# Grouped cross-attention: spreading maxima and sums by VectorE's transposes, and normalising one step later

## The chip, the cores and the metric

The kernel runs on one core of a Trainium2 chip. The metric is the device time in microseconds (us) of one execution; the median of three runs is given. A profile of a further execution gives the order of time on each engine: TensorE (PE, with its weight loads as PEld), VectorE (DVE), ScalarE (ACT), GpSimd (POOL) and the DMA queues.

## The reference

Four cross-attention layers follow each other on a state `x` of 4 batches x 512 queries x 256 channels, with one context of 4 x 1024 keys x 512 channels; everything is float32. Layers 0, 2 and 3 are "masked": 16 heads of 64, logits scaled by 1/8, with 20 subtracted from two pairs of key columns for the queries that a mask names. Layer 1 is "grouped": a norm of the queries, 16 query heads of 16, four of which share one of 4 key heads.

```python
# layers 0, 2, 3
logits = jnp.einsum('bhqd,bhkd->bhqk', q, k) * scale + col_bias[None, None, :, :]
out = jnp.einsum('bhqk,bhkd->bhqd', softmax(logits), v)
x = out.transpose(...).reshape(B, HW, 1024) @ Wo + bo + x
# layer 1
q = (rmsnorm(x, norm_w) @ wq).reshape(B, T, 16, 16); k, v = cond @ wk, cond @ wv   # 4 heads of 16
scores = jnp.einsum('btgrd,bsgd->bgrts', qg, k) * 0.25
x = x + einsum('bgrts,bsgd->btgrd', softmax(scores), v).reshape(B, T, 256) @ wo
```

## The kernel before, in words

**Units and steps.** Each layer of each batch is cut into 8 units, so there are 96 masked and 32 grouped units. A masked unit is two heads; its logits, transposed (keys on partitions, queries along the free dimension), are 8 tiles of 128 keys x (2 heads x 512 queries). A grouped unit is four query heads' half: two of the four sharing groups, its logits again 8 tiles of 128 x 1024. Its index `h` is 0 ("even") or 1 ("odd"); an even and the following odd unit share one output tile `gq[b, "o"]` of 128 x 512. The order is written out by hand in two strings: 96 steps, each with one masked unit `g`, and in 32 of them one grouped unit `lam` as well. The grouped units of a batch stand in eight steps on end; the four batches' runs of eight are apart. In the code of a step, `coming` is the grouped unit of the next step, `follows` the masked one, `g1` the masked unit of the step before.

**One step in order.** `scores(g)` makes the 8 masked logit tiles (L653, one with the mask product L659), ScalarE copies each to SBUF (L663), and VectorE keeps a running maximum in PSUM (L667). `max_quarters` turns and reduces that maximum to one value for each query (L713, L721, L738). With a grouped unit, `reciprocal_sums(g1)` then sums the exponentials of `g1` over the keys and makes its reciprocals (L713 again, L810 to L821). Then four rounds follow on TensorE: two key blocks of `attend(g1)` (L685), then `exponentials_pair(lam, i)`, which is two grouped logit tiles (L617, "pair i") whose exponentials ScalarE takes straight from PSUM (L640). `scale_out(g1)` multiplies the output by its reciprocals (L830), `max_everywhere` spreads the masked maximum over the partitions (L745), and VectorE subtracts it from the 8 tiles (L750), ScalarE exponentiates (L756), GpSimd sums (L795). Beside these, a list `fill` gives TensorE the projections of queries (L549), outputs (L845), keys (L473) and values (L515), attention of the grouped unit (`attend_grouped`), and, between them, the logits of `coming` for its maximum only (`maxima_pair`, L617 with L607 and L609). A step without a grouped unit attends to `g1` in one go after `max_everywhere` and then goes to its list, outputs first. Each engine runs its instructions in the order in which the code issues them.

**The grouped maximum.** After the last of the four `maxima_pair`s, `max_columns` reduces the maxima to columns `mcol` (L713, L721, L730). In the next step, after six of the eight masked score tiles, `lower_queries(lam)` spreads them by 16 products with the identity (L630), and VectorE puts them, negated, into the row of the queries that meets a row of ones in the keys (L635). The grouped logits then come out already lowered by their maximum.

**The grouped sums.** The values carry a column of ones at place 16 of each 32, so the output tile has its sums in row 16 of each 32. At the end of a step with an odd unit, `sums_grouped` spreads these rows by a product with `sel` (L705); `normalise_grouped` turns them, takes reciprocals, turns them back and multiplies (L571 to L573 in `reciprocal_rows`, L800). Its output is projected in the next step.

**PSUM banks.** PSUM's eight banks are handed out by a small class `Place` when the code is built, for one bank or for an aligned pair. Each bank carries the count of returns at which it was last given back; a bank taken is deleted from the dictionary, a bank returned is put at its end with the newest count. A pair goes by the later of its two counts. A single bank goes by this rule:

```python
at = min(free, key=lambda n: free[n] + (2 if n ^ 1 in free else 0))
```

A bank's next user must wait for the last reader of the one before. Pair 0 of the grouped logits takes two aligned pairs while the masked maximum still holds a third and the output of `attend(g1)` one bank of the fourth.

Of the kernel before, what the change touches and what calls it, by code (L numbers as in the profile page):

```python
# [12 lines left out]
ALU = mybir.AluOpType  # L13
# [3 lines left out]
P = 128  # L17
B, S, C = 4, 512, 256
T, CT = 1024, 512
NI = S // P  # L20
NT = T // P
# [55 lines left out]
def kernel(ctx: ExitStack, tc: tile.TileContext, a: dict, out: bass.AP):  # L77
    nc = tc.nc
# [7 lines left out]
    def t_(shape, tag, name, bufs=1, dtype=FP):  # L86
        return sb.tile(shape, dtype, tag=tag, name=name, bufs=bufs)
# [31 lines left out]
    def st_slot(n):  # L119
        return st_all[:, n // (NT + 1), n % (NT + 1), :]  # L120
# [4 lines left out]
    ident = t_([P, P], "ident", "ident")  # L125
# [2 lines left out]
    nc.vector.memset(ones, 1.0)  # L128
    eps = t_([P, 1], "eps", "eps")
    nc.vector.memset(eps, EPS)  # L130

    sel = t_([P, 4, 32], "sel", "sel")
    nc.vector.tensor_copy(
        sel, ident.rearrange("p (g d) -> p g d", d=32)[:, :, 16:17].to_broadcast([P, 4, 32])
    )


    row16 = t_([P, 2], "row16", "row16")
    nc.vector.reduce_sum(
# [316 lines left out]
    gq = {}  # L456
# [108 lines left out]
    def reciprocal_rows(out_, in_, room):  # L565


        turned = room[:, 0:S]
        short = t_([P, S // 32, 1], "short", f"short{len(turns)}")
        turns.append(0)  # L570
        nc.vector.transpose(turned, in_)  # L571
        nc.vector.reciprocal(short, turned.rearrange("p (c r) -> p c r", r=32)[:, :, 0:1])
        nc.vector.transpose(  # L573
            out_.rearrange("p (c r) -> p c r", r=32), short.to_broadcast([P, S // 32, 32])
        )
# [44 lines left out]
                )  # L620
        return ws

    def lower_queries(g):

        w = Place(1)
        m = w.ap
        for n in range(NI):
            for c in range(4):
                column = NI * (c % 2) + n
                nc.tensor.matmul(  # L630
                    m[32 * c : 32 * (c + 1), n * P : (n + 1) * P],
                    lhsT=g.mcol[:, column : column + 1].to_broadcast([P, 32]), rhs=ident,
                    start=True, stop=True,
                )
        nc.vector.scalar_tensor_tensor(g.qt, m, row16[:, 1:2], g.qt, ALU.mult, ALU.add)  # L635
        w.back()

    def exponentials_pair(g, i):
        for odd, w in enumerate(logits_pair(g, i)):
            nc.scalar.activation(g.st[2 * i + odd], w.ap, AF.Exp)  # L640
            w.back()

    def scores(g, within):
        g.st = [st_slot((NT + 1) * g.ring + t) for t in range(NT)]
        g.mx = st_slot((NT + 1) * g.ring + NT)
        g.mx_place = Place()
        for t in range(NT):

            w = Place() if t else g.mx_place
            m = w.ap  # L650
            keys = slice(t * P, (t + 1) * P)
            for j in range(2):
                nc.tensor.matmul(  # L653
                    m[:, j * S : (j + 1) * S], lhsT=g.kt[g.rows[j], keys], rhs=g.qt[g.rows[j], :],
                    start=True, stop=t > 0,
                )
            if t == 0:
                for j in range(2):
                    nc.tensor.matmul(  # L659
                        m[:, j * S : (j + 1) * S], lhsT=aug_k[g.l][g.rows[j], keys],  # L660
                        rhs=aug_q[g.rows[j], :], start=False, stop=True,
                    )
            nc.scalar.copy(g.st[t], m)  # L663
            if t:
                w.back()
                top = g.mx_place.ap
                nc.vector.tensor_tensor(top, top, g.st[t], ALU.max)  # L667
            if t == 5:
                within()

    def place_out(g, width=1):
        g.place = Place(width)
# [26 lines left out]
        nc.vector.tensor_tensor(half, half, g.po[64:128, :], ALU.add)  # L699
        g.place.back()  # L700

    def sums_grouped(g):
        g.place = Place(1)
        g.psum = g.place.ap
        nc.tensor.matmul(  # L705
            g.psum, lhsT=sel.rearrange("p g d -> p (g d)"), rhs=gq[g.b, "o"], start=True, stop=True
        )

    def over_quarter(out_, of, op):
        nc.vector.tensor_reduce(  # L713
            out_, of.rearrange("p (b x) -> p b x", x=32), AX.X, op, apply_transpose=True
        )
# [5 lines left out]
        nc.vector.tensor_tensor(half, quarter[0:64, :], quarter[64:128, :], ALU.max)  # L721
        return half

    def max_columns(g):

        half = max_halves(g, g.mx)
        g.mcol = t_([P, 2 * NI], "mcol", f"mcol_{g.name}", bufs=3)
        of = half.rearrange("x (c h) -> x h c", h=4)
        for h in range(4):
            nc.vector.tensor_tensor(  # L730
                g.mcol[32 * h : 32 * (h + 1), :], of[0:32, h, :], of[32:64, h, :], ALU.max
            )

    def max_quarters(g):
        half = max_halves(g, g.mx_place.ap)
# [6 lines left out]
    def max_everywhere(g):  # L742
        g.mb_place = Place()
        g.mb = g.mb_place.ap
        nc.vector.transpose(  # L745
            g.mb.rearrange("p (b r) -> p b r", r=32), g.every.to_broadcast([P, 2 * S // 32, 32])
        )
# [46 lines left out]
    def running_sum(g, t):  # L794
        nc.gpsimd.tensor_tensor(g.acc, g.st[0] if t == 1 else g.acc, g.st[t], ALU.add)  # L795

    def normalise_grouped(g, room):
        g.ot = t_([P, S], "ot", f"ot_{g.name}", bufs=3)
        reciprocal_rows(g.ot, g.psum, room)
        nc.vector.tensor_tensor(g.ot, gq[g.b, "o"], g.ot, ALU.mult)  # L800
        g.place.back()

    def reciprocal_sums(g):

        w = Place(1)
        quarter, half = w.ap[:, 0:32], w.ap[0:64, 32:64]
        other = t_([64, 32], "other", f"other_{g.name}")
        short = t_([P, S // 32, 1], "short", f"short_{g.name}")
        over_quarter(quarter, g.acc, ALU.add)
        nc.vector.tensor_copy(other, quarter[64:128, :])  # L810
        nc.vector.tensor_tensor(half, quarter[0:64, :], other, ALU.add)
        nc.vector.tensor_copy(other[0:32, :], half[32:64, :])
        for h in range(4):
            cols = slice(h // 2 * S // 32, (h // 2 + 1) * S // 32)
            nc.vector.tensor_tensor(
                short[32 * h : 32 * (h + 1), :, 0], half[0:32, cols], other[0:32, cols], ALU.add
            )
        w.back()
        nc.vector.reciprocal(short, short)
        g.ot = t_([P, S], "ot", f"ot_{g.name}", bufs=3)  # L820
        nc.vector.transpose(  # L821
            g.ot.rearrange("p (c r) -> p c r", r=32), short.to_broadcast([P, S // 32, 32])
        )
# [81 lines left out]
    def at(n):  # L905
        return steps[n] if 0 <= n < len(steps) else (None, None)
# [32 lines left out]
    g0, g1 = masked[0:2]  # L939
# [23 lines left out]
    attended = None  # L963
    count = 0
    ready = []
    left = {b: 32 - 4 for b in range(B)}

    for n in range(len(steps) + 2):
        g, lam = at(n)
        follows, coming = at(n + 1)  # L970
        soon = at(n + 2)[1]
        g1, attended = attended, g
# [42 lines left out]
        def pair(i):  # L1015
            if i == 0:
                behind_exponentials()
            maxima_pair(coming, i)
            if i == NT // 2 - 1:
                max_columns(coming)  # L1020

        if coming:
            share(coming)
# [12 lines left out]

        if g:
            g.now = NT if masked_at(g.n + 1) else 4
            scores(g, lambda: lower_queries(lam) if lam else None)

        ending = n >= len(steps) - 2
        if g1 and (g or lam):
# [1 line left out]
        if g:  # L1044
            max_quarters(g)
            if not lam:
                g.mx_place.back()
                max_everywhere(g)
        if lam:
            if g1:  # L1050
                reciprocal_sums(g1)
            for i in range(NT // 2):
                if g1:
                    attend(g1, range(2 * i, 2 * i + 2))
                if coming and not g:
                    pair(i)
                exponentials_pair(lam, i)
                if i == 0 and g:
                    g.mx_place.back()
                if not g:  # L1060
                    if i == 1 and outs:
                        project_out(outs.pop(0))()
                    if i == 2 and queries:
                        project_q(queries.pop(0))()
            if g1:
                scale_out(g1)
                ready.append(g1)
            if g:
                max_everywhere(g)
        elif g1 and g:  # L1070
            attend(g1)
            if not ending:
                late.append(lambda: normalise(g1))
        elif g1:
            attend_last(g1)
            adds = [project_out(each) for each in outs]
            outs = []
            reciprocal_rows(g1.ot, g1.psum, g1.mx)
            scale_out(g1)
            for add in adds:  # L1080
                add()
# [71 lines left out]
        while pairs:  # L1153
            pair(pairs.pop(0)[1])
        behind_exponentials()
        if coming and not follows:
            lower_queries(coming)
        if lam and lam.h == 1:
            sums_grouped(lam)
            normalise_grouped(lam, st_slot((NT + 1) * (count % 2) + NT))  # L1160
            ready.append(lam)
        if g1 and g1 not in ready:
            ready.append(g1)
# [30 lines left out]
```

## Time and profile before

| what | value |
|---|---|
| median of 3 runs | 3775.26 us (3774.84 to 3775.55) |
| profiled execution | 3773.92 us, span 3772.2 us from the first to the last instruction |
| mean granted TensorE clock | 0.998 |
| busy share: TensorE, VectorE, ScalarE, GpSimd | 99%, 80%, 56%, 43% |
| DMA | 98.71 MB, mean 26 GB/s |

In the profile a group's line gives the line of code, engine, operation, tiles (out<-in) and sizes, then the count, busy time and the mean of one in ns. An fp32 product stands as two matmul records for each product in the code. TensorE's matmuls overlap in the records, so the cost of a block on TensorE is read from its start to the start of what follows.

### The profile page before, as it was taken

To read this page: it belongs to the slowest core of one execution; us is meant where nothing else is said; L and a number is where in the kernel's file an instruction comes from. 1 tells how busy PE (TensorE), PEld (TensorE's weight loads), DVE (VectorE), ACT (ScalarE), POOL (GpSimd) and SP (SyncE) were. 2 spreads that over 40 slices of the span, in tenths; PEclk is the share of its full clock that TensorE was granted. 3 is DMA by queue.
4 is the path that set the end of the run, shared out by engine and by line. 5 is a ranking of instruction groups with operands and counts; after the bars stand their busy time and mean duration, and the time that the engine had idled before them with its cause. 6 is when DMAs were issued, how large, how long until landed. Compare 5 with 4: busy or idle time off the path is not lost.

```text
span 3772.2 us, 50461 instructions
## 1 busy us (share of the span) xinstructions
PE 3723.8 (99%) x19662; PEld 1860.2 (49%) x19662; DVE 3000.4 (80%) x3928; ACT 2104.1 (56%) x2433; POOL 1625.0 (43%) x749
## 2 busy tenths in 40 slices
PE   8999999999999999999999999999999999999998
PEld 4555544445444444444555555554544445555554
DVE  6887787877887778787888888888787778888888
ACT  4555555555555555555555555555555555555554
POOL 3555333343333433333555555555333335555554
PEclk9999999999999999999999999999999999999999
DMA  2111110001000010000000110000100000000100
GB/s 68 42 31 28 39 28 21 18 20 25 22 19 21 12 33 19 22 21 18 26 26 26 43 42 24 25 26 22 26 19 23 20 24 26 26 26 26 31 25 8
DMA packets 187875, 98.71 MB, mean 26 GB/s; under 512 B 43241, under 2 KB 183529, under 8 KB 187637
## 3 DMA queue, kind: packets, MB, share of 16 engines
q1 hardware_dynamic: 182510, 82.90, 8.0%
q0 software_dynamic: 2560, 8.39, 0.8%
q10 hardware_dynamic: 2566, 4.20, 0.5%
q8 instruction: 155, 2.54, 0.3%
q14 instruction: 84, 0.68, 0.1%
HBM read 89.16 MB, written 2.10 MB: 24 GB/s over the span
## 4 chain that ended last, share of the span: by engine, by line
PE 86%; DVE 9%; issue 2%; ACT 2%; DMA 0%; DVEq 0%; POOL 0%; ACTq 0%; POOLq 0%
PE ps L515 19%; PE ps L685 18%; PE ps L473 17%; PE ps L653 12%; PE ps L617 7%; DVE ps L667 6%; PE ps L845 5%; PE ps L549 5%; ACT st L663 2%; DVE st L750 1%; PE ps L491 1%; DVE qt L635 1%; PE ps L659 1%; PE ps L705 0%; PE ps L379 0%
## 5 line engine op out<-in xcount | busy, mean ns | idle before, releaser
L795 POOL TENSOR_TENSOR st<-st 128x1024 f32<-128x1024 f32 x668 | 1580.5, 2366 | 2088.3 <-ACT st L756 2044.0
L667 DVE TENSOR_TENSOR ps<-ps,st 128x1024 f32<-128x1024 f32 x672 | 828.2, 1232 | 462.8 <-ACT st L663 405.5
L756 ACT ACTIVATE st<-st 128x1024 f32<-128x1024 f32 x768 | 783.0, 1054 | 650.0 <-DVE st L750 636.2
L750 DVE TENSOR_TENSOR st<-st,ps 128x1024 f32<-128x1024 f32 x768 | 885.9, 1214 | 3.3
L685 PE MATMUL ps<-st,v 128*64 128x512 f32 x4064 | 810.9, 598 | 0.0
L663 ACT COPY st<-ps 128x1024 f32<-128x1024 f32 x768 | 716.1, 1044 | 107.3 <-PE ps L659 82.3
L515 PEld LDWEIGHTS ps<-wv,ctx 128*128 128x128 f32 x6400 | 729.4, 192 | 80.9 <-issue 64.6
L515 PE MATMUL ps<-wv,ctx 128*128 128x128 f32 x6400 | 744.8, 276 | 0.6 <-ACT st L663 0.6
L653 PE MATMUL ps<-qt,kt 64*128 64x512 f32 x3072 | 710.5, 598 | 0.0
L473 PE MATMUL ps<-ctx,wk 128*128 128x512 f32 x1536 | 693.3, 599 | 2.2 <-ACT ctx L385 2.2
L685 PEld LDWEIGHTS ps<-st,v 128*64 128x64 f32 x4064 | 231.2, 130 | 551.5 <-issue 491.6
L473 PEld LDWEIGHTS ps<-ctx,wk 128*128 128x128 f32 x1536 | 285.7, 190 | 395.7 <-issue 375.0
L653 PEld LDWEIGHTS ps<-qt,kt 64*128 64x128 f32 x3072 | 282.7, 186 | 323.8 <-ACT st L663 142.2
L527 ACT COPY v<-ps 128x512 f32<-128x512 f32 x200 | 117.2, 586 | 538.2 <-PE ps L515 538.1
L609 DVE TENSOR_TENSOR st<-st,ps 128x1024 f32<-128x1024 f32 x224 | 273.5, 1221 | 128.1 <-ACT st L607 70.7
L640 ACT ACTIVATE st<-ps 128x1024 f32<-128x1024 f32 x256 | 248.1, 1021 | 180.2 <-PE ps L617 139.8
L617 PE MATMUL ps<-qt,kt 32*128 32x512 f32 x2048 | 302.6, 639 | 16.1 <-DVE qt L635 12.8
L845 PE MATMUL ps<-ot,wo 128*128 128x512 f32 x448 | 214.6, 607 | 0.7 <-DVE ot L830 0.7
L549 PE MATMUL ps<-x,wq 128*128 128x512 f32 x384 | 185.5, 606 | 1.1 <-ACT x L357 1.1
L617 PEld LDWEIGHTS ps<-qt,kt 32*128 32x128 f32 x2048 | 91.0, 183 | 191.0 <-ACT st L640 52.2
L478 ACT COPY kt<-ps 128x512 f32<-128x512 f32 x192 | 110.3, 574 | 102.8 <-PE ps L473 102.6
L845 PEld LDWEIGHTS ps<-ot,wo 128*128 128x128 f32 x448 | 79.8, 189 | 129.2 <-issue 120.0
(143 smaller groups left out, 1629.9 us busy)
## 6 DMA issues: line engine op xcount, KB each, us to landing
wk<-in_L_xattn_Wk_dram SPq DMA_DIRECT2D x96, 256.0 KB, 2.9
wv<-in_L_xattn_Wv_dram SPq DMA_DIRECT2D x96, 256.0 KB, 2.7
wq<-in_L_xattn_Wq_dram SPq DMA_DIRECT2D x96, 128.0 KB, 2.8
wo<-in_L_xattn_Wo_dram SPq DMA_DIRECT2D x96, 128.0 KB, 2.9
qt<-qt ACTq DMA_DIRECT2D x32, 128.0 KB, 2.2
xraw<-in_x_dram SPq DMA_DIRECT2D x3, 512.0 KB
out_dram<-out SPq DMA_DIRECT2D x3, 512.0 KB
wq<-in_L_xattn_wq_dram SPq DMA_DIRECT2D x32, 32.0 KB, 3.4
```

The costliest lines, as they stand in the source:

```text
L473: nc.tensor.matmul(m, lhsT=g.wk[:, k, :], rhs=ctx_t[g.b][:, k, n * 512 : (n + 1) * 512], start=(k == 0), stop=(k == KT - 1),)
L515: nc.tensor.matmul(m[:, t * P : (t + 1) * P], lhsT=ctx_t[g.b][:, k, (4 * n + t) * P : (4 * n + t + 1) * P], rhs=g.wv[:, k, :], start=(k == ...
L549: nc.tensor.matmul(m, lhsT=g.wq[:, k, :], rhs=x[:, k, :], start=(k == 0), stop=(k == KC - 1))
L617: nc.tensor.matmul(ws[odd].ap[:, j * S : (j + 1) * S], lhsT=g.kt[rows, i * P : (i + 1) * P], rhs=g.qt[rows, :], start=True, stop=True,)
L653: nc.tensor.matmul(m[:, j * S : (j + 1) * S], lhsT=g.kt[g.rows[j], keys], rhs=g.qt[g.rows[j], :], start=True, stop=t > 0,)
L663: nc.scalar.copy(g.st[t], m)
L667: nc.vector.tensor_tensor(top, top, g.st[t], ALU.max)
L685: nc.tensor.matmul(g.po[at, :], lhsT=g.v[:, t, rows], rhs=g.st[t][:, j * S : (j + 1) * S], start=(t == first), stop=(t == last),)
L750: nc.vector.tensor_tensor(g.st[t], g.st[t], g.mb, ALU.subtract)
L756: nc.scalar.activation(st, st, AF.Exp)
L795: nc.gpsimd.tensor_tensor(g.acc, g.st[0] if t == 1 else g.acc, g.st[t], ALU.add)
L845: nc.tensor.matmul(m[:, k * S : (k + 1) * S], lhsT=g.wo[:, k * P : (k + 1) * P], rhs=g.ot, start=True, stop=True,)
```

## The change

The 16 products of the lowering and the product of the sums are taken out, with the tile `sel`. `lower_queries` absorbs `max_columns`: the maxima are put into a tile `every` of 128 x 16 and a VectorE transpose of its broadcast spreads them into a PSUM bank; the lowering of the queries follows at once, now at the end of the step before (after the last `maxima_pair`). `normalise_grouped` turns the output tile itself into a PSUM bank, takes the reciprocals of column 16 of each 32, turns them back into the same bank and multiplies from there. It no longer runs at the end of the odd unit's step: the unit goes into a list `turned`, which the next step empties behind `max_quarters` and, where there is a grouped unit, `reciprocal_sums(g1)`.

```diff
-    def max_columns(g):
+    def lower_queries(g):
         half = max_halves(g, g.mx)
-        g.mcol = t_([P, 2 * NI], "mcol", f"mcol_{g.name}", bufs=3)
-        of = half.rearrange("x (c h) -> x h c", h=4)
-        for h in range(4):
+        every = t_([P, S // 32, 1], "every1", f"every1_{g.name}")
+        for c in range(4):
+            cols = slice(c % 2 * S // 32, (c % 2 + 1) * S // 32)
             nc.vector.tensor_tensor(
-                g.mcol[32 * h : 32 * (h + 1), :], of[0:32, h, :], of[32:64, h, :], ALU.max
+                every[32 * c : 32 * (c + 1), :, 0], half[0:32, cols], half[32:64, cols], ALU.max
             )
+        w = Place(1)
+        m = w.ap
+        nc.vector.transpose(
+            m.rearrange("p (b r) -> p b r", r=32), every.to_broadcast([P, S // 32, 32])
+        )
+        nc.vector.scalar_tensor_tensor(g.qt, m, row16[:, 1:2], g.qt, ALU.mult, ALU.add)
+        w.back()
...
-    def normalise_grouped(g, room):
+    def normalise_grouped(g):
+        o = gq[g.b, "o"]
+        w = Place(1)
+        m = w.ap
+        short = t_([P, S // 32, 1], "short", f"short_{g.name}")
+        nc.vector.transpose(m, o)
+        nc.vector.reciprocal(short, m.rearrange("p (c r) -> p c r", r=32)[:, :, 16:17])
+        nc.vector.transpose(
+            m.rearrange("p (c r) -> p c r", r=32), short.to_broadcast([P, S // 32, 32])
+        )
         g.ot = t_([P, S], "ot", f"ot_{g.name}", bufs=3)
-        reciprocal_rows(g.ot, g.psum, room)
-        nc.vector.tensor_tensor(g.ot, gq[g.b, "o"], g.ot, ALU.mult)
-        g.place.back()
+        nc.vector.tensor_tensor(g.ot, o, m, ALU.mult)
+        w.back()
...
             if i == NT // 2 - 1:
-                max_columns(coming)
+                lower_queries(coming)
...
-            scores(g, lambda: lower_queries(lam) if lam else None)
+            scores(g)
...
             if not lam:
                 g.mx_place.back()
                 max_everywhere(g)
+        if lam and g1:
+            reciprocal_sums(g1)
+        for each in turned:
+            normalise_grouped(each)
+        turned.clear()
         if lam:
-            if g1:
-                reciprocal_sums(g1)
             for i in range(NT // 2):
...
         if lam and lam.h == 1:
-            sums_grouped(lam)
-            normalise_grouped(lam, st_slot((NT + 1) * (count % 2) + NT))
+            turned.append(lam)
             ready.append(lam)
```

More of the change, by code (lines that the diff above doesn't have):

```diff
@@ L130 @@
     nc.vector.memset(eps, EPS)
[L132 to L135, printed above, removed]
     row16 = t_([P, 2], "row16", "row16")
@@ L621, in logits_pair @@
         return ws
[L623 to L636, printed above, removed]
     def exponentials_pair(g, i):
@@ L641, in exponentials_pair, with scores @@
             w.back()
-    def scores(g, within):
+    def scores(g):
         g.st = [st_slot((NT + 1) * g.ring + t) for t in range(NT)]
@@ L667, in scores @@
                 nc.vector.tensor_tensor(top, top, g.st[t], ALU.max)
-            if t == 5:
-                within()
     def place_out(g, width=1):
@@ L700, in keep_odd @@
         g.place.back()
[L702 to L707, printed above, removed]
     def over_quarter(out_, of, op):
@@ L965 @@
     ready = []
+    turned = []
     left = {b: 32 - 4 for b in range(B)}
@@ L1155 @@
         behind_exponentials()
-        if coming and not follows:
-            lower_queries(coming)
         if lam and lam.h == 1:
-            sums_grouped(lam)
-            normalise_grouped(lam, st_slot((NT + 1) * (count % 2) + NT))
+            turned.append(lam)
             ready.append(lam)
```

## The prediction

> **What bounds the kernel now.** I read the busy table first, then the chain of waits on TensorE, then the order of time around one step that has a grouped unit in it.
>
> ```profile
> PE 3723.8 (99%) x19662; PEld 1860.2 (49%) x19662; DVE 3000.4 (80%) x3928; ACT 2104.1 (56%) x2433; POOL 1625.0 (43%) x749
> ```
>
> TensorE is busy 3723.8 of 3772.2 us; all its idle time together is 48 us. What is taken off TensorE is gained, and what makes it wait is lost. The removed work in the groups (busy us, mean ns), and TensorE's largest wait:
>
> ```profile
> L630 PE MATMUL ps<-ident,mcol 128*32 128x128 f32 x1024 | 34.6, 276 | 0.0
> L705 PE MATMUL ps<-o,sel 128*128 128x512 f32 x32 | 16.4, 594 | 0.0
> ...
> PE ps L617 <- DVE qt L635: 12.8, 32, 0.7
> ```
>
> The timeline of TensorE at one step boundary (start us, length):
>
> ```profile
> 520.49 1.02 PE L705 MATMUL ps<-o,sel 128*128 128x512 f32 x2
> 521.44 1.13 PE L653 MATMUL ps<-qt,kt 64*128 64x512 f32 x4
> ...
> 527.00 1.08 PE L630 MATMUL ps<-ident,mcol 128*32 128x128 f32 x32
> 528.01 1.99 PE L653 MATMUL ps<-qt,kt 64*128 64x512 f32 x8
> 529.93 1.94 PE L685 MATMUL ps<-st,v 128*64 128x512 f32 x8
> 532.16 1.14 PE L617 MATMUL ps<-qt,kt 32*128 32x512 f32 x8 [0.29 <-DVE qt L635]
> ```
>
> Starts are what count: L705 costs 521.44 - 520.49 = 0.95 us, the L630 block 528.01 - 527.00 = 1.01 us. L617 at 532.16 is pair 0 of the grouped exponentials. VectorE at the same boundary:
>
> ```profile
> 521.83 0.72 DVE L571 STREAM_TRANSPOSE st<-ps 128x512 f32<-128x512 f32 x1
> 522.58 0.25 DVE L572 RECIPROCAL short<-st 128x16 f32<-128x16 f32 x1
> 522.87 0.71 DVE L573 STREAM_TRANSPOSE ot<-short 128x512 f32<-128x512 f32 x1
> 523.62 0.69 DVE L800 TENSOR_TENSOR ot<-o,ot 128x512 f32<-128x512 f32 x1
> 524.78 6.58 DVE L667 TENSOR_TENSOR ps<-ps,st 128x1024 f32<-128x1024 f32 x5 [0.47 <-ACT st L663]
> ...
> 534.52 1.25 DVE L713 TRANSPOSE_TENSOR_REDUCE quarter<-ps 128x32 f32<-128x1024 f32 x1
> ...
> 539.76 0.71 DVE L821 STREAM_TRANSPOSE ot<-short 128x512 f32<-128x512 f32 x1
> ```
>
> The grouped normalising (L571 to L800) takes 524.31 - 521.83 = 2.48 us and now lies in a gap: the next L667 waits for ScalarE anyway. VectorE's tree, from the first L667 to L821's end at 540.47, runs 8.3 us past pair 0's start on TensorE. That lead of TensorE over VectorE is what the change touches.
>
> [...] The trace agrees: each engine's lines stand in the order of the code. So one waiting matmul holds everything behind it. [...] The trace shows it once, at the start, in a table of windows (PEclk is the granted clock):
>
> ```profile
> 12.00:16.00 4.00, 0.57 (x2) 0.14 (x1) 0.54 (x3) 0.60 (x1) 3.09 (x4) 0.90 0.54 141
> 16.00:20.00 4.00, 3.06 (x13) 2.66 (x14) 3.83 (x8) 1.01 (x1) 3.08 (x4) 0.50 0.70 204
> ```
>
> With 0.57 us of matmuls in 4 us the clock fell to 0.50, and came back near 25 us.
>
> **The change, part by part.** A unit is even (h=0) or odd (h=1); 32 units are lowered, 16 pairs are normalised.
>
> *Removed from TensorE.* Lowering: 32 x 1.01 = 32.3 us. Sums: 16 x 0.95 = 15.2 us. The wait of pair 0 for L635: 12.8 us, gone because the queries are lowered at the end of the step before. Together -60.3 us.
>
> *Lowering on VectorE.* It adds a transpose to PSUM, 128x512; the nearest row, L573 to SBUF, has 0.71 us, half of L745 to PSUM 0.63, so 0.72 is safe. The four small maxima stay (L730 163 ns, L815 of the new width 165 ns). 32 x 0.72 = 23 us more VectorE, at a point where it has slack, except one: the lowering's bank goes, by the allocator's rule, to the third score tile of the next step. Behind an odd unit L730 ends at 521.81; transpose and L635 bring that to 523.30. The scores start 0.95 us earlier, at 520.49, and their third tile 2.04 us later (aug product included), 522.53. TensorE waits 0.8 us there, in 12 steps. Behind an even unit the lowering is done before that tile, by 1.1 us or more. The tile `sel` costs 0.3 us once in the setup: nothing. No DMA is issued, dropped or moved past another; SP's, POOL's and ScalarE's orders stay.
>
> *Normalising a step later.* Its four instructions cost what they did (0.72 + 0.25 + 0.71 + 0.69 and gaps, 2.48 us; PSUM instead of SBUF for the turned copy changes a few 10 ns: L571 reading PSUM has 716). But they now stand behind `max_quarters` and `reciprocal_sums`, and take a PSUM bank. Which one decides all. At that point two banks hold the maximum; three pairs were last returned by score tiles 5, 6 and 7, say at counts 1, 2 and 3. `place_out` takes one bank of the oldest pair; `reciprocal_sums` takes that bank's neighbour and returns it at count 4. Now the rule "least recent, plus 2 if the neighbour is free too" gives tile 6's banks 2 + 2 = 4, tile 7's 5, and the lone neighbour 4. A tie: `min` takes the first in the dictionary's order, and a returned bank is put last. So the normalising takes **a bank of tile 6's pair**. The pair-0 logits then need both remaining pairs, and their second place contains that bank: its matmul must wait until the last multiply of the normalising has read it.
>
> *The price.* From the scores' start: a step without a lowering in it shows when the tree comes (at 813.56 the scores start, L713 at 826.25), +12.69. L713 to L821's end is 540.47 - 534.52 = 5.95; normalising 2.51 with a gap; a semaphore 0.06; the third tile's delay passes on 0.3. Sum +21.5. TensorE reaches pair 0 at 532.16 - 521.44 - 1.01 - 0.29 = +9.4. It loses **12.1 us** (0.8 of it at the third tile), in every step whose predecessor had an odd unit and that has a grouped unit itself: 3 for each of 4 batches, 12. 12 x 12.1 = 145 us. Behind pair 0 stand attention, projections and keys, all later by as much; everybody else waits for them. Pair 1's later half now stalls 0.26 us for ScalarE's first exponentials (L617 at 535.10 takes 1.40, not 1.14); with pair 0 split in time this goes: -3 us.
>
> *The clock.* [...] I take 2.4[...]: 12 x 2.4 = 29 us (20 to 41; 0 if the clock held).
>
> *Last pair of each batch.* The next step has no grouped unit. There L745 ends at 829.95, and L800 would end at 832.46; the second project-out (L845, block 827.86 to 831.40, half of it is 1.77) needs it at 829.63. 2.9 us x 4 = 12 us.
>
> *Sum.* -60.3 + 145 - 3 + 29 + 12 = +123 us. The profiled execution has 3773.92 us (span 3772.2), so 3897; the median of the runs stands 1.3 us above it: 3898.
>
> **Rivals.**
> *The normalising's bank is not in pair 0's way* (the tie falls to the neighbour, or the bank is the next user's and late). Then -60.3 + 12 x 0.8 + 12 = -39, 3736; up to 12 x 2.5 us more if the delay of L830 behind the normalising shows, 3766. For it: of the five banks that neither the maximum nor the attention holds, one, the lone neighbour, is not used by pair 0, and it loses only by the tie. Against it: the counts above. It decides at a single point: whether any matmul before the fourth attention block needs that bank.
> *The stall comes but the clock holds*: 3869. Against it: the drop at 15 us above.
> *The loss is partly recovered* by waits that TensorE has anyway: they are 48 us in all, half of them at the two ends, so not below about 3845.
> *The change does not do what it says*: were the tree still limited by products, L705 would stay; nothing in the diff leaves one.
> *VectorE becomes the bound of whole steps*: 37.59 us busy in a step of 49.00; 3 us more do not fill it.
>
> **How the numbers follow.** Stall with the lower clock 0.78; stall without it or partly recovered 0.09; no collision 0.11, nearly all of it faster; a net near zero 0.02. A change of 0.2% (7.6 us) is about what a measurement can tell. So faster 0.11, same 0.02, slower 0.87. The range leaves out the no-collision case; it goes from partial recovery, 3845, to the clock's upper bound with some us of tree on top, 3925.
>
> **What would show it.** Right: TensorE (or its weight load) waits about 11 us, 12 times, on the last multiply of the grouped normalising; the clock shows halves there, mean below 0.99; L630's and L705's groups and the wait for L635 are gone; the projections of four steps wait 3 us. Wrong: no wait over 1 us on that multiply, pair 0 at +9.4 us after its scores, time near 3736.

## The result, and the profile after

The changed kernel takes 3901.2 us (median of 4 runs, 3898.9 to 3902.3) against 3775.2 us before: a ratio of 1.033, 95% interval 1.0315 to 1.0351. It is 126 us slower; the prediction said 3898, 123 slower. Its profiled execution has 3898.92 us, span 3897.1 us, 124.9 us more than the span before.

The busy table of the profile after:

```profile
PE 3721.6 (95%) x18606; PEld 1840.1 (47%) x18606; DVE 3025.9 (78%) x3959; ACT 2109.1 (54%) x2433; POOL 1625.3 (42%) x749
```

TensorE has 1056 matmul records fewer (the removed products), yet its busy time is only 2 us less: some of what remains ran slower, at a mean granted clock of 0.977 (0.998 before). Its share of the span fell from 99% to 95%. The waits of TensorE, longest first (us in total, times, longest):

```profile
PE ps L611 <- DVE ot L787: 122.8, 12, 10.2
PE ps L832 <- issue: 10.3, 4, 2.6
PE ps L632 <- DVE qt L709: 7.8, 12, 0.7
```

L611 is the grouped logits (L617 before), L787 the last multiply of the grouped normalising (L800 before): the twelve waits that the prediction named. L832 is the projection of the last pair of each batch; the profile names no releaser for it, but it starts at 857.59, 0.10 us behind the end of that pair's last multiply (856.80 + 0.69). L632 is a masked score tile that waits for the lowering's bank. The wait for the lowered queries (12.8 us before, at L635) is gone. The same step as the one shown before, on TensorE:

```profile
516.87 1.13 PE L632 MATMUL ps<-qt,kt 64*128 64x512 f32 x4
...
519.71 5.42 PE L632 MATMUL ps<-qt,kt 64*128 64x512 f32 x24 [0.64 <-DVE qt L709]
525.06 1.94 PE L662 MATMUL ps<-st,v 128*64 128x512 f32 x8
526.93 1.13 PE L611 MATMUL ps<-qt,kt 32*128 32x512 f32 x4
538.28 2.08 PE L611 MATMUL ps<-qt,kt 32*128 32x512 f32 x4 [10.22 <-DVE ot L787]
540.29 3.65 PE L662 MATMUL ps<-st,v 128*64 128x512 f32 x8
543.87 1.14 PE L611 MATMUL ps<-qt,kt 32*128 32x512 f32 x8
```

The first half of pair 0 starts at 526.93, the second, whose place holds the normalising's bank, 11.35 us later. Then the attention block L662 takes 3.65 us where the same eight records took 1.94 before. And on VectorE, what TensorE waited for:

```profile
529.91 1.25 DVE L683 TRANSPOSE_TENSOR_REDUCE quarter<-ps 128x32 f32<-128x1024 f32 x1
...
535.13 0.71 DVE L808 STREAM_TRANSPOSE ot<-short 128x512 f32<-128x512 f32 x1
535.77 0.68 DVE L781 STREAM_TRANSPOSE ps<-o 128x512 f32<-128x512 f32 x1
536.49 0.26 DVE L782 RECIPROCAL short<-ps 128x16 f32<-128x16 f32 x1
536.78 0.73 DVE L783 STREAM_TRANSPOSE ps<-short 128x512 f32<-128x512 f32 x1
537.54 0.69 DVE L787 TENSOR_TENSOR ot<-o,ps 128x512 f32<-128x512 f32 x1
```

The tree (L683 to L808), then the normalising, ends at 538.23; TensorE resumes at 538.28. The table of windows around it (PEclk behind POOL's column):

```profile
530.00:538.00 8.00, 0.00 (x0) 0.00 (x0) 7.48 (x20) 0.00 (x0) 0.00 (x0) 0.51 0.00 0
538.00:543.00 5.00, 4.72 (x12) 1.27 (x12) 0.23 (x1) 1.03 (x1) 0.00 (x0) 0.50 0.00 0
543.00:548.00 5.00, 5.00 (x30) 1.23 (x28) 0.00 (x0) 1.94 (x2) 0.00 (x0) 0.92 0.00 0
857.00:861.00 4.00, 3.41 (x5) 1.38 (x6) 4.00 (x5) 1.14 (x2) 0.00 (x0) 0.60 0.00 0
```

From 528.06 to 538.28 no matmul runs, neither L611's nor any of the blocks behind it; the granted clock is 0.50 for some 5.5 us behind the wait. In the last line, at the end of the first run of grouped steps, a wait of only 2.6 us is followed by a lowered clock as well (0.60 in the mean of these 4 us).

### The profile page after: what moved, and what is told of

It is laid out like the page before. It is cut to its first block, busy times and chain, and to the rows that moved or that the text cites. A ratio compares the mean times of both kernels' runs of the same rounds, so it can differ in the third digit from the quotient of the medians.

```text
span 3897.1 us, 48391 instructions
## 1 busy us (share of the span) xinstructions
PE 3721.6 (95%) x18606; PEld 1840.1 (47%) x18606; DVE 3025.9 (78%) x3959; ACT 2109.1 (54%) x2433; POOL 1625.3 (42%) x749
## 4 chain that ended last, share of the span: by engine, by line
PE 87%; DVE 10%; ACT 1%; issue 1%; DMA 0%; POOL 0%; DVEq 0%; ACTq 0%; POOLq 0%
PE ps L662 19%; PE ps L509 17%; PE ps L467 17%; PE ps L632 14%; PE ps L611 7%; PE ps L832 5%; PE ps L543 5%; DVE ps L646 4%; DVE st L728 1%; DVE quarter L683 1%; DVE st L603 1%; ACT st L642 1%; PE ps L485 1%; DVE ps L683 1%; PE ps L638 0%
## 5 line engine op out<-in xcount | busy, mean ns | idle before, releaser
L734 ACT ACTIVATE st<-st 128x1024 f32<-128x1024 f32 x768 | 786.5, 1056 | 660.0 <-DVE st L728 644.5
L728 DVE TENSOR_TENSOR st<-st,ps 128x1024 f32<-128x1024 f32 x768 | 886.4, 1217 | 3.2
L662 PE MATMUL ps<-st,v 128*64 128x512 f32 x4064 | 829.6, 608 | 0.0
L632 PE MATMUL ps<-qt,kt 64*128 64x512 f32 x3072 | 705.0, 597 | 7.8 <-DVE qt L709 7.8
L467 PE MATMUL ps<-ctx,wk 128*128 128x512 f32 x1536 | 693.5, 599 | 2.2 <-ACT ctx L379 2.2
L662 PEld LDWEIGHTS ps<-st,v 128*64 128x64 f32 x4064 | 234.6, 131 | 568.6 <-issue 485.9
L467 PEld LDWEIGHTS ps<-ctx,wk 128*128 128x128 f32 x1536 | 286.0, 190 | 396.8 <-issue 377.6
L611 PE MATMUL ps<-qt,kt 32*128 32x512 f32 x2048 | 325.3, 653 | 126.0 <-DVE ot L787 122.8
L632 PEld LDWEIGHTS ps<-qt,kt 64*128 64x128 f32 x3072 | 284.1, 186 | 334.6 <-ACT st L642 156.4
L611 PEld LDWEIGHTS ps<-qt,kt 32*128 32x128 f32 x2048 | 93.6, 187 | 317.0 <-DVE ot L787 132.7
L832 PE MATMUL ps<-ot,wo 128*128 128x512 f32 x448 | 221.3, 622 | 11.0 <-issue 10.3
L817 DVE TENSOR_TENSOR ot<-ps,ot 128x512 f32<-128x512 f32 x96 | 66.4, 692 | 142.9 <-PE ps L662 138.5
```

Source lines behind the costliest of these rows:

```text
L467: nc.tensor.matmul(m, lhsT=g.wk[:, k, :], rhs=ctx_t[g.b][:, k, n * 512 : (n + 1) * 512], start=(k == 0), stop=(k == KT - 1),)
L611: nc.tensor.matmul(ws[odd].ap[:, j * S : (j + 1) * S], lhsT=g.kt[rows, i * P : (i + 1) * P], rhs=g.qt[rows, :], start=True, stop=True,)
L632: nc.tensor.matmul(m[:, j * S : (j + 1) * S], lhsT=g.kt[g.rows[j], keys], rhs=g.qt[g.rows[j], :], start=True, stop=t > 0,)
L662: nc.tensor.matmul(g.po[at, :], lhsT=g.v[:, t, rows], rhs=g.st[t][:, j * S : (j + 1) * S], start=(t == first), stop=(t == last),)
L728: nc.vector.tensor_tensor(g.st[t], g.st[t], g.mb, ALU.subtract)
L734: nc.scalar.activation(st, st, AF.Exp)
```

## The experiments

The theory: the loss is one PSUM bank, shared by the normalising and the second half of pair 0, and the clock that falls in the wait. The rivals: the normalising's 2.5 us on VectorE in front of the steps that follow, or the lowering's added VectorE work. Times of the kernel before in the three groups of runs were 3774.8, 3775.2 and 3775.3 us.

**The other side of the tie.** The changed kernel, in which the normalising takes the lone bank:

```diff
+            if lone and any(n ^ 1 not in free for n in free):
+                at = max(n for n in free if n ^ 1 not in free)
...
-        w = Place(1)
+        w = Place(1, lone=True)
```

> The changed kernel, but the normalising takes the lone bank beside the attention's output (the other side of the tie). Theory 'bank': the 12 waits of pair 0 (11.3 us and 2.65 us of halved clock each) go, 3901 - 12 x 14 = 3733; the query projection of L543 now gets that bank and waits some 1.5 us for it 12 times, so about 3751. Rival 'the normalising's 2.5 us on VectorE, in front of the output's scaling and the subtractions, are what costs': the bank does not matter, 3880 or more.

Measured: 3751.9 us, ratio to before 0.9937 (0.9921 to 0.9954). One bank number changes a kernel that is 3.3% slower into one that is 0.6% faster. The twelve long waits are gone; the query projection has its new one, at 1.1 us rather than 1.5 (ten times as below, and twice, at 1.2 us, without a named releaser):

```profile
PE ps L545 <- DVE ot L789: 11.3, 10, 1.1
```

That 3751 was met so closely is in part luck: the first pair of maxima is late here too, which was not counted (at 650.90 it takes 1.71 us from start to start, and 1.07 in the kernel before).

**No bank at all.** The normalising turns in SBUF, in its own output tile:

```diff
-        w = Place(1)
-        m = w.ap
+        g.ot = t_([P, S], "ot", f"ot_{g.name}", bufs=3)
+        m = g.ot
```

> The changed kernel, but the normalising turns in SBUF, in its own output tile, and takes no PSUM bank; instructions, order and place the same. Theory 'bank': 3901 - 12 x 14 = 3733, no wait of TensorE over 1 us on the normalising inside the runs of eight steps; the four waits of the projections at the ends of the runs stay (2.6 us and a short halving of the clock each). Rival 'VectorE's time': 3880 or more.

Measured: 3754.7 us, ratio 0.9948 (0.9932 to 0.9965). The bank's theory holds in the main: 146 us are gone, more than the net loss of 126, with the instructions, their order and their place kept. But 3733 was missed by 22 us. From one mask product to the next, the twelve even steps behind an odd one took on average 1.0 us more than before, where -1.0 was expected. TensorE has new waits there, at most 0.7 us each:

```profile
PE ps L611 <- DVE st L728: 4.2, 6, 0.7
PE ps L467 <- DVE st L728: 4.1, 6, 0.7
```

L728 is VectorE's subtraction of the spread maximum. The bank of that maximum comes free with the last one, and the first pair of maxima (L611) takes it. These 8.3 us are only the idle time that the profile lists. The two halves of the pair, which otherwise overlap (both together take 1.07 us from start to start, in other steps one alone 1.05), now follow each other: in the step where the pair starts at 649.00, what follows it starts 2.88 us later, against 1.07 us in the kernel before. So the rival of VectorE's time is not the main loss, but it is not nothing either: VectorE's chain has become a second bound in these steps.

**The lowering alone**, on the kernel before:

```diff
-                max_columns(coming)
+                lower_queries(coming)
...
-            if t == 5:
-                within()
```

> The kernel before with the first part of the change alone: maxima spread by the transpose and lowered a step earlier; sums by the product and normalised at the step's end as before. Theory: 32 x 1.01 of products, 12.8 us of waits and 32 x 0.26 us of pair 1's stall go, -53; the normalising now stands behind the lowering and its bank, which the fourth score tile takes next, comes about 1.35 us late 12 times, +16: 3738. Rival 'VectorE's added transposes cost as much as they save': 3775 or more.

Measured: 3729.5 us, ratio 0.9878 (0.9862 to 0.9895). This half of the change is a gain of 45 us, 8 more than expected (though pair 1's stall, which the expectation counted among the gains, stays). The even steps without a grouped step before them and the odd ones take 1.7 us less each, 34 us in 20 steps. The twelve even steps behind an odd one gain only 0.8 on average. The delay did not lie at the fourth score tile, where it was expected; that tile does not wait. It lies at the first pair of maxima. Before, and in this kernel, the pair and what follows it, in the same step on TensorE:

```profile
554.86 1.14 PE L617 MATMUL ps<-qt,kt 32*128 32x512 f32 x8
555.93 1.98 PE L473 MATMUL ps<-ctx,wk 128*128 128x512 f32 x4
```

```profile
549.69 2.13 PE L617 MATMUL ps<-qt,kt 32*128 32x512 f32 x8
551.74 1.98 PE L473 MATMUL ps<-ctx,wk 128*128 128x512 f32 x4
```

From start to start 1.07 us became 2.05: the wait is inside the group. A weight load of the second half shows what ended it, the subtraction again:

```profile
550.68 0.30 PEld L617 LDWEIGHTS ps<-qt,kt 32*128 32x128 f32 x4 [0.70 <-DVE st L741]
```

**The wait filled.** The changed kernel, with ten products added in each of the twelve waits:

```diff
         for odd in range(2):
+            for _ in range(filled if odd else 0):
+                nc.tensor.matmul(ws[1].ap[:, S:], lhsT=ident, rhs=g.qt, start=True, stop=True)
...
+        filled = 10 if turned else 0
...
-                exponentials_pair(lam, i)
+                exponentials_pair(lam, i, filled if i == 0 else 0)
```

> The changed kernel with ten products of 128x128x512 added in each of the 12 waits of pair 0, into the bank's neighbour, whose results are overwritten (8.6 us of work in a wait of 10.2). Theory 'part of the loss is the clock': [...]the clock stays at 1.0 behind it, 12 x 2.65 = 32 us less than the changed kernel: 3869, and the short drops at the ends of the four runs of steps stay. If the clock had no share: 3901.

Measured: 3875.6 us, ratio 1.0262 (1.0245 to 1.0279), 26 us less than the changed kernel, with more work on TensorE. In its timeline the wait is still there:

```profile
528.07 1.13 PE L613 MATMUL ps<-qt,kt 32*128 32x512 f32 x4
529.12 8.85 PE L610 MATMUL ps<-qt,ident 128*128 128x512 f32 x20
539.42 1.13 PE L613 MATMUL ps<-qt,kt 32*128 32x512 f32 x4 [1.45 <-DVE ot L789]
540.48 1.94 PE L664 MATMUL ps<-st,v 128*64 128x512 f32 x8
```

The second half still starts 11.35 us after the first, but the attention block behind it takes its 1.94 us, with a granted clock of 1.00 from 538 to 543. So the clock is a separate part of the loss. The 7 us that are missing to 3869: in the profiled execution (mean granted clock 0.994) the clock halved for 3.4 us behind 4 of the 12 waits, although only 1.45 us of them were idle, at 1.65 us each. Behind the one that ends at 1151.09, for one, the attention block takes 3.15 us and the next pair 1.57, where they take 1.94 and 1.14 behind the one shown.

**The normalising alone**, with the lowering by products as before (the second half of the diff):

> The kernel before with the second part of the change alone: no product for the sums, normalising in a PSUM bank behind the next step's tree; lowering by 16 products as before. By the same rule of banks the normalising again takes a bank of pair 0. Theory 'bank': 16 x 0.95 = 15 us of products go; pair 0, at 9.8 us after the mask product, waits until the normalising's end at 18.1 + 2.5, so 10.8 us and 2.6 us of halved clock, 12 times, +161 less 3 for pair 1; 4 x 4.5 at the ends of the runs: 3936. Rival 'the lowering on VectorE makes the tree late, and that is the loss': this kernel is near 3775.

Measured: 3941.3 us, ratio 1.0439 (1.0422 to 1.0456). The lowering is not what makes pair 0 wait:

```profile
PE ps L617 <- DVE ot L799: 115.4, 12, 9.6
```

The whole loss of the change is in this half, +166 us; the lowering brings back 40.

**Neither part in a bank** (the first two lines are in `lower_queries`; `normalise_grouped` is as in the kernel with no bank for it), and the last pair of each batch normalised at its own step's end:

```diff
-        w = Place(1)
-        m = w.ap
+        m = g.mx[:, 0:S]
...
-            turned.append(lam)
+            if coming:
+                turned.append(lam)
+            else:
+                normalise_grouped(lam)
```

> Both parts of the change with neither taking a bank (the lowering turns in the slot of the maximum, the normalising in its output tile), and the normalising of a run's last unit at its step's end, where VectorE had 10 us idle. Against the kernel with the normalising in SBUF: the ends of the runs lose their waits (-14 us) and the third tile its wait (-8 us, if nothing later takes it back). Theory 'VectorE's chain from the step's boundary to its last subtraction now bounds the 12 even steps behind an odd one': the 8 us come back at the first pair of maxima, which waits for the bank of the spread maximum: 3740. Rival 'TensorE alone bounds': 3732 or less.

Measured: 3739.9 us, ratio 0.9908 (0.9891 to 0.9924). Most of what was taken away at the score tile (7.8 us) came back at the pair of maxima: the two waits for the subtraction grew from 8.3 to 14.9 us:

```profile
PE ps L611 <- DVE st L726: 7.5, 6, 1.2
PE ps L467 <- DVE st L726: 7.4, 6, 1.2
```

But that the time came out at 3740 is in part luck. In the profiled execution (mean granted clock 0.996) the clock halved behind four of these twelve waits, for 3.4 us twice and 6.8 us twice, which the expectation did not hold. One of the four, where L467 takes 3.55 us instead of 1.98:

```profile
645.08 1.13 PE L611 MATMUL ps<-qt,kt 32*128 32x512 f32 x4
647.45 1.22 PE L611 MATMUL ps<-qt,kt 32*128 32x512 f32 x4 [1.24 <-DVE st L726]
648.60 3.55 PE L467 MATMUL ps<-ctx,wk 128*128 128x512 f32 x4
```

These four steps took 2.1 to 4.1 us more than before, the two others with the same wait 0.8 us each. So the lowered clock cost some 9 us; without it the time would be near 3731, and the number alone would have spoken for the rival. The waits speak for VectorE's chain, and the last experiment tests it directly.

**The normalising at its old place**, still without a product and without a bank:

```diff
-            if coming:
-                turned.append(lam)
-            else:
-                normalise_grouped(lam)
+            normalise_grouped(lam)
```

> As the kernel with neither part in a bank, but the normalising stays at the end of the odd unit's own step, as before the change; there is no product for the sums. Against the kernel with the lowering alone (3729.5) 16 products of 0.95 us are gone. Theory 'VectorE's chain bounds the 12 even steps behind an odd one': only the 4 at the ends of the runs pay, 3726. Rival 'TensorE alone bounds': 15 us less, 3714.

Measured: 3727.4 us, ratio 0.9873 (0.9856 to 0.9889). Sixteen products of 0.95 us less than with the lowering alone are worth 2 us, too little to tell from nothing with the intervals of the two. Against the lowering alone the odd steps, in which the product stood, take 0.9 us less each on average, and the twelve even steps behind an odd one 0.9 us more: removing work from TensorE bought nothing where VectorE's chain sets the end.

**The second projection last**, which takes an addition of 1.22 us out of that chain:

```diff
+        last = fill[1:] if lam else []
+        fill = fill[: len(fill) - len(last)]
...
+        fill += last
```

> As the kernel with neither part in a bank and the normalising at its old place (3727.4), but in the steps with a grouped unit the second output projection, which is that of the grouped pair, goes to the end of the list; its addition on VectorE (1.22 us) no longer stands in front of the last subtractions. Theory 'VectorE's chain up to the last subtraction bounds the 12 even steps behind an odd one, by the bank of the spread maximum': up to 1.2 us less in each, about 3714. Rival 'that chain does not bound them': 3727.

Measured: 3716.3 us (3716.1 to 3716.9), ratio 0.9845 (0.9831 to 0.9859): 11 us less, 0.9 on average in each of the twelve even steps behind an odd one, and no wait for the subtraction is left among TensorE's largest. TensorE's order changes too, but a key block takes the place of the projection: in the step looked at, the first pair of maxima starts 32.2 us behind the scores in both kernels, while VectorE's last subtraction ends 32.5 us behind them instead of 33.7. This is the fastest version: 59 us under the kernel before, 185 under the changed one.

## Why the prediction was right, point by point

- *Removed from TensorE.* Right, and a little short: an even step with no grouped unit before it takes 1.69 us less (1.43 were counted), an odd one 2.55 (2.38). The 0.26 us of the even step stand in front of pair 0: without a wait it comes 9.15 us behind the scores' start (in the kernel with the normalising at its old place), where 9.4 was counted. The last two score tiles, for one, took 1.92 us behind the 16 products and take 1.81 without them, so the block of products cost more than from its start to the next. Over the 20 steps that are not stalled it makes some 4 us more gain than said, in the twelve stalled ones some 3. Pair 1's stall of 0.26 us went in the twelve stalled steps, as foreseen, and stayed in the others.
- *The bank.* Right. Followed through a step, the rule in the kernel's code gives the normalising a bank of the sixth tile's pair, the second half of pair 0 waits for it, and the experiment with the other side of the tie shows that nothing else about the normalising costs as much.
- *The price.* The normalising was to end 21.4 us behind the scores' start and to be seen 0.06 later; it ended at 538.23 - 516.87 = 21.36, and TensorE resumed 0.05 later. TensorE reached pair 0 at +10.06, so the third tile cost 10.06 - 9.15 = 0.9 us (0.8 foreseen; the profile lists 0.64 of it as idle). With the 11.35 us at pair 0 the two waits cost 12.3 us (12.1 foreseen).
- *The clock.* Right in kind and near in size: in the step shown 5.6 us from the release to pair 1 instead of 2.94, so 2.65 us. The 2.4 foreseen, with its range, was my estimate; the trace of the kernel before did not show it. In the twelve steps the half clock lasted 4.2 to 6.5 us behind the release. The filled wait shows it apart from the wait.
- *Together* the twelve steps took 12.93 us more than before, 155 us; the prediction's terms for such a step come to 12.1 + 2.4 - 0.26 - 1.01 - 0.29 = 12.9.
- *Last pair of each batch.* The term that was too small: 4.5 us each and not 2.9. The delay itself was as foreseen: from start to start the second projection came 853.03 to 857.59, 4.56 us instead of 1.77, so 2.8 us (2.6 of it listed as idle). But the clock fell behind it too (0.50 for 3.4 us; the second half of the projection took 3.34 us from start to start instead of 1.77), and the prediction put nothing into this term for that. With the normalising in SBUF these steps took 2.9 us more, about the delay alone. The difference is 6 us, and the waits and the clock of the twelve steps are some 5 us above the prediction; the some 7 us more gain above cancel most of it. That the sum is off by only 3 us is in part luck.
- *The rival without collision.* Its 3736 was given a top of 3766 for a normalising that delays VectorE. The two kernels without the collision took 3752 and 3755: half of that top was real. The prediction named the delay of the output's scaling, and the runs showed where it is felt: at the bank of the spread maximum, more than 10 us further on (in the kernel with neither part in a bank the scaling starts at 634.11 and TensorE waits until 647.45).

## What to carry to other kernels

Where buffers are handed out by a rule, a moved instruction is also a new user: write down which buffer it will get and who takes that buffer next, since here one tie in the rule was worth 150 us and 2.5 us of VectorE work cost nothing like it. A wait on the bounding engine that sits behind another engine's whole chain is priced by that chain's end, and on TensorE by the slow clock behind it as well (here 2.65 us behind a wait of 10.2). When TensorE gains a step's worth of work, look for the engine that had been just ahead of it: the next gain lies there, as 1.22 us moved out of VectorE's chain in each grouped step were worth 11 us, and 16 products of 0.95 us taken off TensorE 2 us.

## What the runs showed of the hardware

TensorE's clock fell after waits much shorter than the 11 us that I had priced. The counts that follow are of one profiled execution for each kernel. In the changed kernel 3.4 us at 0.50 came with the wait of 2.6 us at the last pair of a batch in 4 of 4 cases. In the filled waits 1.45 us of idle time were followed by it in 4 of 12, with neither part in a bank 1.2 us in 4 of 12.

The length of the wait alone does not decide, then: of two filled waits, each with 1.45 us idle, the one that ends at 1151.09 was followed by an attention block of 3.15 us instead of 1.94, and the one that ends at 539.42 by a clock of 1.00. What else decides was not tested. In the twelve waits of the changed kernel, each with 10.2 us idle, the clock fell 1.5 to 4.4 us behind the last matmul, and came back within 4.2 to 6.5 us of work, 5.5 in the step shown.
